# More slack for seven kinds of step in a list-scheduled graph network kernel

## The chip, the cores and the metric

The kernel runs on one core of a Trainium2 chip. The time is the device time of one execution in microseconds, as the median of several runs. Five engines take part, each with its own in-order queue of instructions: TensorE (PE in the profile, its weight loads PEld), VectorE (DVE), ScalarE (ACT), GpSimd (POOL) and SyncE (SP, which here only issues DMAs).

## The reference

There are 16 batches of 1024 nodes with 64 channels and one 1024 x 1024 adjacency matrix each. Four layers follow each other, each of the form `x = layernorm(x + layer(x))`:

```python
x = _layernorm(x + _L0_gnn_ref(x, adj, nodemask, ...))   # quantiles over the neighbours, then an MLP
x = _layernorm(x + _L1_gnn_ref(x, adj, weight, bias))    # adj @ (x @ weight) + bias
x = _layernorm(x + _L2_gnn_ref(x, adj, W1, W2, GCN_W))   # (softmax(x W (x W)^T) + adj) @ x, gelu
x = _layernorm(x + _L3_gnn_ref(x, adj, nodemask, ...))   # quantiles again
```

The quantile layers are the costly ones. For each node with more than 10 neighbours the edges whose rank is one certain multiple are removed, from both sides. What is left gives a list of neighbours for each node. For each node and channel the values of the neighbours are sorted, and the quantiles 0.25, 0.5 and 0.75, each interpolated between two ranks, are added with weights 0.25, 0.5 and 0.25.

## The kernel before

The kernel sorts, for each batch, the nodes by degree. The nodes of highest degree (the first 128, the hubs) have long lists; the other 896 have at most 22 neighbours, by 128-node tiles with capacities 22, 16, 13, 11, 10, 9 and 8 (`TILE_CAPS`).

Seven streams of work, written as Python generators, are merged into one program by `give_out` (line 211). A stream yields one instruction at a time, a `Step`. Each step has an engine, a cost from a table of estimates (`Queue.times`, line 183), and the names of the tiles it reads and writes. At every turn `give_out` looks at the next step of each stream, works out when its inputs are ready and when its engine is free by these estimates, and gives out the one that would start first. `.after(slack)` adds to the ready time for this choice alone: the step counts as ready that many nanoseconds later, so other streams' steps on the same engine go ahead of it if they have some, and the estimated start that is booked does not hold the slack. The order in which steps are given out is the order of each engine's queue; the semaphores between engines follow from it. As all instructions are emitted from the helper at line 180, nearly every line of the profile reads L180, and groups are told apart by tile names.

The streams:

- `graph_stream` (1657): for each batch `graph` (964). `neighbours` (994) loads the matrix by tiles, turns it, counts degrees into `pm` and computes `mi` (half the degree) from it. Then a loop over 8 tiles follows: `counted(t)` gives the running count of neighbours by matmuls into `pq`, ScalarE takes `v` = |pq + mid|, VectorE tests it into `gone`, and further matmuls subtract and transpose `gone`. `both_ways` and `order` make the symmetric graph and the order by degree. `lists` (1102) makes the neighbour lists: 32 tests `hot` for the hubs, whose result is `k.hidx`; for each of the 7 tiles of short lists, matmuls into `pk`, from which VectorE takes the 8 greatest keys at a time (`top`, `rest`) into `k.idx`. The graphs of batches run up to `KEPT` = 5 ahead.
- `fetch_stream` (1287), all of GpSimd: per layer 60 gathers of hub rows (`hrows`, 30 pairs, in 8 buffers), 89 gathers of short-list rows (`rows0`, `rows1`, `rows2`, one buffer each), and 9 scatters of the layer's sums (`sums`), those of one layer in the midst of the next layer's gathers.
- `turn_stream` (1323): transposes each pair of hub rows on TensorE into a bank `turned`, four pairs to a bank, and ScalarE copies the bank to `cols`. At the end of a layer it transposes `tot`, the hubs' result, to `hagg`.
- `sort_stream` (1377), VectorE: sorting networks of `min` and `max` over `cols` (the hubs; weighted sums of them give `tot`), then over `rows0` to `rows2`.
- `pick_stream` (1391): ScalarE scales the sorted rows by the quantile weights, TensorE adds them up in `picked`, and ScalarE copies to `agg`.
- `weight_stream` (1355): loads of the hubs' weights, `hw`.
- `middle_stream` (1639): what follows the quantiles. `last_step` (1519) loads `sums` as `ag`, adds x, transposes by halves (`ot`), runs the two MLP matmuls (`ht`, then into `py`), and makes `z`, the mask and the norm from `py` on VectorE. For the first quantile layer the two middle layers follow (`spread_layer`, `attention_layer`), whose result x3 goes to the table that the second quantile layer gathers from. `layernorm` (942) has one step on ScalarE, the square root `ln_r`, whose result VectorE inverts into `ln_q`.

The 32 quantile layers (two for each batch) are run through in one sequence, the second layer of a batch `LAG` = 2 batches after its first.

Of the kernel before, what the change touches and what calls it, by code (L numbers as in the profile page):

```python
# [16 lines left out]
ALU = mybir.AluOpType  # L17
# [766 lines left out]
def listed_path(ctx: ExitStack, tc: tile.TileContext, x, adj, nodemask,  # L784
# [3 lines left out]
    B, N, C = x.shape  # L788
    H = l0_w1.shape[1]
    P = 128  # L790
    NT = N // P
# [3 lines left out]
    V, A, T, G = nc.vector, nc.scalar, nc.tensor, nc.gpsimd  # L795
# [10 lines left out]
    ident = const.tile([P, P], F32, name="ident")  # L806
# [129 lines left out]
    V, A, T, G, D = (Queue(c, e) for c, e in zip("VATGD", (nc.vector, nc.scalar, nc.tensor, nc.gpsimd, nc.sync)))  # L936
# [5 lines left out]
    def layernorm(z, sq, y):  # L942
        s = small["t"].tile([P, NT], F32, name="ln_s")
        yield V.tensor_reduce(s, z, AX.X, ALU.add)
        mean = small["t"].tile([P, NT], F32, name="ln_mean")
        yield V.tensor_scalar(mean, s, 1.0 / C, None, ALU.mult)
        yield V.tensor_tensor(z, z, mean.unsqueeze(2).to_broadcast([P, NT, C]), ALU.subtract)
        yield V.tensor_mul(sq, z, z)
        v = small["t"].tile([P, NT], F32, name="ln_v")
        yield V.tensor_reduce(v, sq, AX.X, ALU.add)  # L950
        yield V.tensor_scalar(v, v, 1.0 / C, EPS, ALU.mult, ALU.add)
        r = small["t"].tile([P, NT], F32, name="ln_r")
        yield A.activation(r, v, AF.Sqrt)

        q = small["t"].tile([P, NT], F32, name="ln_q")
        yield V.reciprocal(q, r)
        yield V.tensor_mul(q, q, v)
        yield V.tensor_add(q, q, r)
        yield V.tensor_scalar(q, q, 0.5, None, ALU.mult)
        yield V.reciprocal(q, q)  # L960
        yield V.tensor_mul(y, z, q.unsqueeze(2).to_broadcast([P, NT, C]))
        return y
# [31 lines left out]
    def neighbours(np, psn, b, k, near, nbt):  # L994
        k.adjt = dram.tile([NH, NT, P, HALF], F32, name="adjt", bufs=3)
        for t in range(NT):
            mine = slice(t * P, (t + 1) * P)
            a = np.tile([P, N], F32, name="a", bufs=3)
            yield D.dma_start(a, adj[b, mine, :])
            nb = np.tile([P, N], F16, name="nb", tag="h", bufs=3)  # L1000
            yield V.tensor_scalar(nb, a, 0.0, None, ALU.is_gt)
            yield V.tensor_mul(nb[:, mine], nb[:, mine], noteye)
            pa = two(psn, [P, NT, P])
            for j in range(NT):
                yield T.transpose(pa[:, j, :], a[:, j * P:(j + 1) * P], ident)
            at = np.tile([P, NT, P], F32, name="at", bufs=2)
            yield A.copy(at, pa)
            h, c0 = t // (HALF // P), t % (HALF // P) * P
            yield A.dma_start(k.adjt[h, :, :, c0:c0 + P].rearrange("j p n -> p j n"), at)
            pb = psn.tile([P, NT, P], F16, name="one")  # L1010
            for j in range(NT):
                yield T.transpose(pb[:, j, :], nb[:, j * P:(j + 1) * P], ident16)
            yield A.copy(nbt[:, :, mine], pb)
        pm = psn.tile([P, NT], F32, name="one")
        for t in range(NT):
            for j in range(NT):
                yield T.matmul(pm[:, t:t + 1], nbt[:, j, t * P:(t + 1) * P], ones16[:, 0:1],
                         start=(j == 0), stop=(j == NT - 1))


        mi = small["g"].tile([P, NT], I32, name="mi")
        yield V.tensor_scalar(mi, pm, 1.0, None, ALU.add)
        do = small["g"].tile([P, NT], F32, name="do")
        yield V.scalar_tensor_tensor(do, pm, 10.0, k.mask, ALU.is_gt, ALU.mult)
        yield V.tensor_scalar(mi, mi, 1, None, ALU.logical_shift_right)
        mid = small["g"].tile([P, NT], F32, name="mid")
        yield V.tensor_scalar(mid, mi, -1.5, -1024.0, ALU.mult, ALU.add)
        off = small["g"].tile([P, NT], F32, name="off")
        yield V.tensor_scalar(off, mi, 0.5, 1.0, ALU.mult, ALU.add)
        yield V.tensor_mul(off, off, do)  # L1030
        yield V.tensor_scalar(off, off, -1.0, None, ALU.add)
        def counted(t):
            pq = two(psn, [P, NH, HALF])
            for h in range(NH):
                last = (h + 1) * (HALF // P) - 1
                for j in range(last + 1):
                    c0 = max(j * P, h * HALF)
                    yield T.matmul(pq[:, h, c0 - h * HALF:], nbt[:, j, t * P:(t + 1) * P],
                                   run[:, c0 - j * P:(h + 1) * HALF - j * P], start=(j == 0), stop=(j == last))
            return pq  # L1040

        pq = yield from counted(0)
        for t in range(NT):
            mine = slice(t * P, (t + 1) * P)
            v = np.tile([P, N], F16, name="v", tag="h", bufs=3)
            yield A.activation(v, pq.rearrange("p h n -> p (h n)"), AF.Abs, bias=mid[:, t:t + 1])
            gone = np.tile([P, N], F16, name="gone", tag="h", bufs=3)
            yield V.tensor_scalar(gone, v, off[:, t:t + 1], None, ALU.is_equal)
            if t + 1 < NT:
                pq = yield from counted(t + 1)  # L1050

            for h in range(NH):
                pn = psn.tile([P, HALF], F32, name="one")
                yield T.matmul(pn, neg16, gone[:, h * HALF:(h + 1) * HALF], start=True, stop=False)
                for j in range(HALF // P):
                    yield T.matmul(pn[:, j * P:(j + 1) * P], nbt[:, h * (HALF // P) + j, mine], ident16,
                                   start=False, stop=(j == HALF // P - 1))
                yield A.copy(near[:, t, h * HALF:(h + 1) * HALF], pn)
            pg = psn.tile([P, NT, P], F16, name="pg", tag="one")
            for j in range(NT):  # L1060
                yield T.transpose(pg[:, j, :], gone[:, j * P:(j + 1) * P], ident16)
            yield A.copy(nbt[:, :, mine], pg)
# [39 lines left out]
    def lists(lp, psl, b, near, perm, deg, k):  # L1102
# [35 lines left out]
        pi = psl.tile([CH, 2, 2 * HC], F32, name="pi", tag="one")  # L1138
# [9 lines left out]
        pi = psl.tile([P, 2, NG], F32, name="pi2", tag="one")  # L1148
        for q in range(GC):
            yield T.matmul(pi, quarter[:, q], named.rearrange("s h (g q) -> s q h g", q=GC)[:, q],  # L1150
                           start=(q == 0), stop=(q == GC - 1))
        yield V.tensor_copy(k.hidx, pi)
        events.add(("hidx", b))


        for g in range(1, NT):
            pk = psl.tile([P, NH, HALF], F32, name="two")
            for h in range(NH):
                cols = slice(h * HALF, (h + 1) * HALF)
                yield T.matmul(pk[:, h], ones16[0:1, :], key_row[:, cols], start=True, stop=False)  # L1160
                for t in range(NT):
                    yield T.matmul(pk[:, h], perm[:, t, g * P:(g + 1) * P], near[:, t, cols],
                             start=False, stop=(t == NT - 1))
            cap = TILE_CAPS[g - 1]
            top = lp.tile([P, MOST + 2], F32, name="top", bufs=2)
            keys = pk.rearrange("p h n -> p (h n)")
            for r in range((cap + 7) // 8):
                yield V.max(out=top[:, 8 * r:8 * r + 8], in_=keys)
                if 8 * r + 8 < cap:
                    rest = lp.tile([P, N], F32, name="rest", bufs=2)  # L1170
                    yield V.match_replace(out=rest, in_to_replace=top[:, 8 * r:8 * r + 8], in_values=keys,
                                    imm_value=-4096.0)
                    keys = rest
            yield V.tensor_scalar(k.idx[:, g - 1, :cap], top[:, :cap], 0.0, None, ALU.max)
# [148 lines left out]
    def turn_stream():  # L1323
        for n, (l, b) in enumerate(layers):
            k = batches[b]
            yield Wait("hidx", b)
            k.cols = [None, None]
            for g in range(0, NG, 4):
                pt = psh.tile([P, 4 * P], F32, name="turned")
                for i in range(g, min(g + 4, NG)):  # L1330
                    yield Wait("h", n, i)
                    e = min(P, (2 * HC - i * GC) * CH)
                    yield T.transpose(pt[:, (i - g) * P:(i - g) * P + e], k.hrows[i][:e].rearrange("p h c -> p (h c)"),
                                      ident[:e, :e]).after(3000)
                events.add(("turned", n, g // 4))
                first, end = g * GC, min((g + 4) * GC, 2 * HC)
                for i in range(2):
# [181 lines left out]
    def last_step(n, l, b, k):  # L1519
# [21 lines left out]
                c0 = t % (HALF // P) * P  # L1541
                yield T.matmul(py[:, t, :], ht[:, c0:c0 + P], w2, start=True, stop=True)
        z = features("z")
        yield V.tensor_tensor(z, py, b2.unsqueeze(1).to_broadcast([P, NT, C]), ALU.add)
        yield V.tensor_mul(z, z, k.mask.unsqueeze(2).to_broadcast([P, NT, C]))
        yield V.tensor_add(z, z, xn)
        return (yield from layernorm(z, ag, features("y")))
# [166 lines left out]
```

## Time and profile before

| | us |
|---|---|
| median of 3 runs | 8266.02 |
| lowest and highest | 8259.21 and 8276.33 |
| the profiled execution | 8298.99 |
| its span, first to last instruction | 8297.2 |

| engine | busy, us | share of the span |
|---|---|---|
| TensorE | 5196.2 | 63% |
| VectorE | 7057.9 | 85% |
| ScalarE | 2329.8 | 28% |
| GpSimd | 5693.1 | 69% |

The mean granted clock of TensorE was 0.738 of full speed. A layer takes 232 to 262 us after the first two, told by the first gather of each layer's hub rows; layers with graph work beside them alternate between about 236 and 260 us, and those after the last graph (from 7000 us on) take 226 to 247 us.

A line of groups gives: engine, operation, out<-in by tile names, shapes and count; then busy time in us and the mean of one in ns; then the engine's idle time ahead of these instructions in us and what ended most of it. A line of waits gives: who waited, for whom, how long in total, how many times, and the longest. A line of the timeline gives start, length, engine, instruction, and in brackets the idle time ahead of it and its releaser.

### The profile page before, as it was taken

The numbers are of one execution on the slowest core, as the hardware profiler recorded it, in microseconds if no ns is written. First come the engines' busy times: TensorE is split into PE (matmuls) and PEld (weight loads), VectorE is DVE, ScalarE is ACT, GpSimd is POOL, SyncE is SP. The second block draws the span as 40 slices with busy tenths as digits, with TensorE's granted clock in tenths as the row PEclk, the third lists the DMA queues.
The fourth block names the chain that finished last, engine by engine and source line by source line (L and its number), as shares of the span: only waits on it lengthen the run. The fifth ranks groups of instructions, "written<-read, shape, count | busy, mean of one in ns | idle before, by whom it ended". The sixth has DMA issues, their size and how long they took to land. (4 is left out here: it accounts for less than half of the span.)

```text
span 8297.2 us, 81388 instructions
## 1 busy us (share of the span) xinstructions
PE 5196.2 (63%) x24851; PEld 2751.4 (33%) x24851; DVE 7057.9 (85%) x14774; ACT 2329.8 (28%) x5554; POOL 5693.1 (69%) x5087
## 2 busy tenths in 40 slices
PE   6568777758475675856658575665856668272541
PEld 4244333333332333433233333323333233131221
DVE  2779798789898898988889898898988889979795
ACT  3324334142322324132242313324232232121121
POOL 0734677667776776767767676777767777777774
PEclk8778887878686776877778686777867678565565
DMA  1331423232323222232322324222332222232221
GB/s 48 72 72 50 99 44 97 46 77 65 73 50 89 52 55 69 62 81 52 63 63 66 73 50 94 52 51 69 72 71 52 65 61 65 33 68 33 58 42 22
DMA packets 762008, 513.78 MB, mean 62 GB/s; under 512 B 459098, under 2 KB 600538, under 8 KB 761306
## 3 DMA queue, kind: packets, MB, share of 16 engines
q1 hardware_dynamic: 457434, 261.99, 13.0%
q0 software_dynamic: 161792, 163.90, 11.6%
q10 hardware_dynamic: 142336, 82.59, 3.4%
q8 instruction: 201, 3.29, 0.2%
q14 instruction: 245, 2.01, 0.1%
HBM read 408.73 MB, written 103.55 MB: 62 GB/s over the span
## 5 line engine op out<-in xcount | busy, mean ns | idle before, releaser
L180 POOL DMA_INDIRECT rows<-table,idx x2848 | 3264.6, 1146 | 867.9 <-issue 841.1
L180 POOL DMA_INDIRECT hrows<-table,hidx x1920 | 2096.4, 1092 | 928.8 <-issue 443.1
L180 DVE TENSOR_TENSOR spare<-cols 128x528 f32<-128x528 f32 (+11 forms) x1632 | 1057.1, 674 | 71.4 <-ACT cols L180 47.7
L180 DVE TENSOR_TENSOR cols<-spare 128x528 f32<-128x528 f32 (+11 forms) x1664 | 1074.8, 680 | 15.8
L180 PE MATMUL picked<-rows,ident 128*128 128x64 f32 (+2 forms) x2496 | 646.1, 366 | 347.6 <-ACT rows L180 346.6
L180 PE MATMUL turned<-ident,hrows 128*128 128x128 f32 x960 | 343.1, 379 | 673.6 <-DMA hrows<-table,hidx 636.3
L180 POOL DMA_INDIRECT sums<-agg,node x224 | 260.2, 1162 | 665.2 <-DMA sums<-agg,node 195.3
L180 ACT ACTIVATE rows<-rows,wt 128x64 f32<-128x64 f32 x2272 | 612.5, 340 | 191.2 <-DVE rows L180 188.5
L180 PEld LDWEIGHTS picked<-rows,ident 128*128 128x128 f32 x2496 | 479.7, 244 | 543.1 <-ACT rows L180 446.3
L180 PE MATMUL pi<-hot,numbers 128*32 128x236 f16 x4096 | 549.4, 284 | 76.0 <-DVE hot L180 74.4
L180 DVE TENSOR_TENSOR spare<-rows 128x64 f32<-128x64 f32 (+8 forms) x1056 | 539.0, 541 | 58.1 <-DMA sums<-hagg,hnode 21.7
L180 PE MATMUL two<-near,perm 128*128 128x512 f16 x1792 | 544.6, 459 | 0.0
L180 PEld LDWEIGHTS <-numbers 128*32 128x32 f16 x4096 | 397.0, 103 | 331.8 <-issue 275.7
L180 ACT COPY cols<-turned 128x512 f32<-128x512 f32 (+3 forms) x288 | 148.5, 528 | 1253.8 <-PE turned L180 1252.9
L180 PE MATMUL two<-run,nbt 128*128 128x512 f16 (+3 forms) x1536 | 408.9, 438 | 142.4 <-ACT v L180 142.4
L180 PEld LDWEIGHTS turned<-ident,hrows 128*128 128x128 f32 x960 | 163.4, 175 | 926.5 <-issue 591.9
L180 PEld LDWEIGHTS <-nbt 128*128 128x128 f16 x3584 | 303.6, 113 | 491.4 <-issue 416.9
L180 DVE TENSOR_TENSOR rows<-spare 128x512 f32<-128x512 f32 (+9 forms) x896 | 462.5, 538 | 0.8
L180 PE MATMUL turned<-ident,tot 128*64 128x128 f32 x32 | 11.7, 365 | 609.4 <-DVE tot L180 609.4
L180 DVE TENSOR_TENSOR spare<-cols,spare 128x472 f32<-128x472 f32 (+2 forms) x704 | 379.2, 539 | 15.6
L180 PE MATMUL one<-xt,wt 64*128 64x512 f32 x512 | 369.8, 851 | 22.0 <-DVE top L180 22.0
L180 DVE TENSOR_TENSOR rows<-rows,spare 128x64 f32<-128x64 f32 (+4 forms) x1120 | 363.2, 329 | 17.6
(232 smaller groups left out, 10079.9 us busy)
## 6 DMA issues: line engine op xcount, KB each, us to landing
at<-adjt SPq DMA_DIRECT2D x512, 256.0 KB
a<-in_adj_dram SPq DMA_DIRECT2D x128, 512.0 KB
adjt<-at ACTq DMA_DIRECT2D x128, 512.0 KB
rows<-table,idx POOLq DMA_INDIRECT x2848
hrows<-table,hidx POOLq DMA_INDIRECT x1920
hw<-hwt SPq DMA_DIRECT2D x64, 472.0 KB
hwt<-ho ACTq DMA_DIRECT2D x64, 236.0 KB
ag<-sums SPq DMA_DIRECT2D x32, 256.0 KB
```

The source lines that it names most:

```text
L180: return Step(lambda: f(*args, **kw), self.engine, cost, late, reads, writes, "dma" in name)
```

## The change

The change adds a slack to six kinds of VectorE steps, and doubles the slack that the hub transpositions already had on TensorE. Nothing else differs.

```diff
@@ layernorm
-        yield V.reciprocal(q, r)
+        yield V.reciprocal(q, r).after(1000)
@@ neighbours
-        yield V.tensor_scalar(mi, pm, 1.0, None, ALU.add)
+        yield V.tensor_scalar(mi, pm, 1.0, None, ALU.add).after(3000)
...
-            yield V.tensor_scalar(gone, v, off[:, t:t + 1], None, ALU.is_equal)
+            yield V.tensor_scalar(gone, v, off[:, t:t + 1], None, ALU.is_equal).after(2000)
@@ lists
-        yield V.tensor_copy(k.hidx, pi)
+        yield V.tensor_copy(k.hidx, pi).after(3000)
...
-                yield V.max(out=top[:, 8 * r:8 * r + 8], in_=keys)
+                yield V.max(out=top[:, 8 * r:8 * r + 8], in_=keys).after(0 if r else 1500)
@@ turn_stream
                     yield T.transpose(pt[:, (i - g) * P:(i - g) * P + e], k.hrows[i][:e].rearrange("p h c -> p (h c)"),
-                                      ident[:e, :e]).after(3000)
+                                      ident[:e, :e]).after(6000)
@@ last_step
-        yield V.tensor_tensor(z, py, b2.unsqueeze(1).to_broadcast([P, NT, C]), ALU.add)
+        yield V.tensor_tensor(z, py, b2.unsqueeze(1).to_broadcast([P, NT, C]), ALU.add).after(6000)
```

## The prediction

> **What bounds the kernel now.** I read the busy shares first, then the idle time of VectorE by group, then the waits of VectorE and GpSimd in the even middle of the run (1000 to 6750 us, which is 1380 of the 1920 hub gathers, so 23 of 32 layers, 250 us each), and last one wait in the timeline.
>
> ```profile
> PE 5196.2 (63%) x24851; PEld 2751.4 (33%) x24851; DVE 7057.9 (85%) x14774; ACT 2329.8 (28%) x5554; POOL 5693.1 (69%) x5087
> ...
> L180 POOL DMA_INDIRECT rows<-table,idx x2848 | 3264.6, 1146 | 867.9 <-issue 841.1
> L180 POOL DMA_INDIRECT hrows<-table,hidx x1920 | 2096.4, 1092 | 928.8 <-issue 443.1
> ```
>
> VectorE leads, but GpSimd is as full as it: beside 5693 us busy it has 841 + 443 us of "issue", about 0.3 us ahead of each gather, in which it waits for nothing. Together 84%.
>
> ```profile
> L180 DVE TENSOR_SCALAR gone<-v,off 128x1024 f16<-128x1024 f16 x128 | 65.1, 509 | 251.1 <-ACT v L180 251.1
> L180 DVE TENSOR_TENSOR z<-one,b 128x512 f32<-128x512 f32 x32 | 22.1, 689 | 222.0 <-PE one L180 222.0
> L180 DVE MAX8 top<-two 128x8 f32<-128x1024 f32 x112 | 137.6, 1228 | 151.7 <-PE two L180 151.6
> L180 DVE CAST hidx<-pi 128x60 uint32<-128x60 f32 x16 | 3.5, 219 | 53.2 <-PE pi L180 53.2
> L180 DVE TENSOR_SCALAR mi<-one 128x8 int32<-128x8 f32 x16 | 2.6, 162 | 26.9 <-PE one L180 26.9
> L180 DVE RECIPROCAL ln_q<-ln_r 128x8 f32<-128x8 f32 x64 | 12.4, 193 | 15.3 <-ACT ln_r L180 15.3
> ```
>
> VectorE's idle time is 8297 − 7058 = 1239 us; 720 us of it stand ahead of these six groups, and they are the six VectorE steps that the change defers. For rows that GpSimd has to fetch VectorE waits next to nothing, so sorting work is nearly always there to fill a gap.
>
> ```profile
> POOL sums L180 <- DMA sums<-agg,node: 135.9, 74, 3.2
> POOL hrows L180 <- PE turned L180: 124.8, 63, 23.7
> POOL sums L180 <- ACT agg L180: 90.1, 16, 12.6
> POOL sums L180 <- DMA sums<-hagg,hnode: 70.1, 23, 5.4
> POOL hrows L180 <- DMA hrows<-table,hidx: 57.6, 189, 0.3
> POOL sums L180 <- ACT rows L180: 48.4, 27, 9.2
> ```
>
> These are GpSimd's waits from 1000 to 6750 us. The scatters wait for each other (136 + 70) and keep doing so. What a faster VectorE can give back: 209 us for late sorts and picks (90 + 48, and in the rest of that view 29 + 15 + 13 + 8 + 4 + 1 on VectorE's rows, cols, spare, z, top and hd) and 139 us for hub buffers not yet turned (125 + 14). So GpSimd cannot get under 5750 − 348 = 5402 us there, 235 us a layer.
>
> ```profile
> 4104.30 0.45 PE L180 MATMUL turned<-ident,hrows 128*128 128x128 f32 x1 [2.73 <-DMA hrows<-table,hidx]
> 4107.32 0.44 PE L180 MATMUL turned<-ident,hrows 128*128 128x128 f32 x1 [2.58 <-DMA hrows<-table,hidx]
> 4110.32 0.45 PE L180 MATMUL turned<-ident,hrows 128*128 128x128 f32 x1 [2.56 <-DMA hrows<-table,hidx]
> 4113.55 0.47 PE L180 MATMUL turned<-ident,hrows 128*128 128x128 f32 x1 [2.78 <-DMA hrows<-table,hidx]
> ...
> 4127.04 0.69 DVE L180 TENSOR_TENSOR z<-one,b 128x512 f32<-128x512 f32 x1 [14.13 <-PE one L180]
> ```
>
> Here is the worst wait: the last step's matmuls stand on TensorE behind hub transpositions that wait, one by one, for gathers 2.5 to 3 us apart; 14 us later z can start, and VectorE stood still for it. Twelve of the 32 z waits are of 14 to 18 us, 179 us together.
>
> **The change, part by part.** No instruction is added or removed; instructions of each kind are as many in both built programs, table loads of ScalarE (50) too. GpSimd's stream is a single one and keeps its order. What moves is the order on VectorE, TensorE, ScalarE and SyncE. For the VectorE steps I counted, in both built orders, the VectorE work that stands between the producer and the step, with durations from the trace's groups (a 128x512 f32 operation 0.68 us, and so on), and took from each traced wait the added cover, never more than the wait.
>
> Graph test (gone): cover 1.3 us before, 2.8 after; a traced wait is 251/128 = 2.0 us. Instance by instance 127 us go. The eight tests of the first graph wait 8 us each with nothing else to run and keep it.
>
> z: cover 0.9 before, 6.2 after. That alone takes 94 us (222 to 128; the last z, 13 us, has no cover). But the transpositions' larger slack acts on the same wait: between the add of ag and z stand 18 hub transpositions in every other layer before, 7 after. In the stretch above, five of them cost 13.4 us between ot (done at 4102.3) and the next matmul (4115.7); after, one stands there. I take 195 us: all but the last z and some 14 us. Bounds 94 and 209.
>
> First maximum (top): cover 0.3 to 1.4; 27 us, of 152, since the slack only helps where hub or sorting work is ready and the first graph (about 30 us) has none. As TensorE will stand less behind waiting transpositions I take 45; bounds 27 and 120.
>
> hidx 29 us (cover 0.5 to 2.8), mi 18 (0.4 to 3.0), ln_q 11 (0.5 to 1.5).
>
> Hub transpositions: TensorE waits 636 us for their gathers. The order has 5 gathers (median) between a row pair's second gather and its transposition before, 7 after: 2 x (1.09 + 0.3) = 2.8 us more. At a mean wait of 636/351 = 1.8 us most of these waits go. TensorE is at 63%, so this is worth nothing by itself beyond z and top. Its price: 8 row-pair buffers are 16 gathers, the transposition has 7 instead of 9 gathers' time (9.7 for 12.5 us) before the refill is held up.
>
> Late next: hidx is 400 us or more ahead of its first gather from the sixth batch on (at 4406 us for a layer whose gathers begin at 4821); in batches 1 and 2 only 27 us, where the order leaves VectorE's work ahead of it unchanged or 8 us less. The x3 that follows z is some 470 us ahead of its layer, in the last one 32 us: there the tail can gain no more than that. SyncE's loads move too; VectorE waits for them 45 us (nb) and 19 us (ag), nearly all before 100 us and at the end: 0 ± 20. ScalarE is busy for 28%; its copies to cols, which wait 1253 us for TensorE, come later with the transpositions and so hold up the row scalings behind them less: again 0, and up to 20 us either way.
>
> Sum on VectorE: 127 + 195 + 45 + 29 + 18 + 11 = 425 us, bounds 306 and 514.
>
> Of this the span gets what GpSimd can follow. In the middle 366 of VectorE's 557 us of waits go, two thirds. Late sorts also move up: the last operation of a network stands 7 to 18 us of VectorE work earlier in most layers, because graph work is put behind it. So I let 80% of the 209 us go, 167; of the 139 us for hub buffers 40%, since VectorE's tot comes sooner but the transpositions themselves later: 55. That is 222 us, 240 us a layer. From 6750 us on GpSimd has 45 us of such waits: 20. From 0 to 1000 us, where the graph sets the pace, 35 of VectorE's 56 us after the first graph. Sum 277.
>
> The profiled execution took 8299.0 us (span 8297.2), 33 us over the median of the runs, 8266.0. 8299 − 277 = 8022, or 3.3% less; on the median 7990.
>
> One more price: gathers take 940 ns at best and 1146 in the mean. If that difference comes from a busy VectorE, 425 us less idle time touch 425/1.45 = 293 gathers with 0.2 us, 60 us on GpSimd; if not, 0. I take 0 and keep 60 for the range. The Trainium skill (SBUF — State Buffer, "Who interferes with whom") speaks against the change here: a VectorE operation in a two-port mode locks GpSimd out while it makes descriptors. By the same section tensor_tensor, which is what fills the gaps, has no such mode, so its price would be 0; by the row above it would be up to 60 us, 8050 for 7990.
>
> **The rivals.** *GpSimd follows wholly:* all 348 us of the middle go, 60 elsewhere: 408, 7860. For it: 94% of GpSimd's middle is already work. Against: two engines bound through eight buffers and one set of rows each never both run without waits.
>
> *GpSimd binds at once:* VectorE's waits go, but hub buffers come free later and only the 209 us shrink, by half: 105 and 25 elsewhere, 130: 8136. For it: TensorE waits 344 us in the middle for tot, 15 times and 23 us each, over the 9.7 us that the buffers bear.
>
> *Slower:* TensorE's long graph strings push each deferred group of four transpositions past the buffers' 9.7 us, and GpSimd stops for 2.8 us more each time. There are 32 x 15 = 480 groups; it decides from 277/2.8 = 99 of them. At one in four, 120 x 2.8 = 336: 59 us slower, 8325. Against: GpSimd now meets "PE turned" 99 times with 177 us, and that wait is TensorE's for tot, which comes earlier.
>
> *Nothing is ready when steps are deferred,* so the order stays: 8266. The built order speaks against it, except for the first graph.
>
> **How the numbers follow.** Forecast 7990 (7900 to 8080): 0.52. GpSimd follows wholly: 0.14. It binds at once: 0.20. No change, 0.2% or 17 us either way, which is about what this kernel's measurement can tell: 0.03. Slower: 0.11. Faster is 0.86. The range 7850 to 8200 leaves out the far part of the first rival, the weak end of the second, and the slower case.
>
> **What would show it.** Right: idle ahead of gone near 125 us, z under 40, top near 100; TensorE's wait for hub gathers well below 636; layers of 240 us in the middle; GpSimd's waits on ACT agg and rows down to a fifth. Wrong: "hrows <- PE turned" above 177 us by hundreds (the slower case), or VectorE's idle time moved to waits for rows or cols (GpSimd binds).

## The result: 0.5% slower

| | before | after |
|---|---|---|
| median, us (7 runs each) | 8266.99 | 8318.82 |
| lowest and highest | 8258.16 and 8280.46 | 8294.75 and 8327.80 |
| the profiled execution, and its span | 8298.99, 8297.2 | 8327.80, 8326.0 |

The ratio is 1.005, with a 95% interval of 1.0037 to 1.0062. The forecast was 7990 us. The traced execution of before was 32 us above its median and that of after 9 us above, so the traces differ by 29 us where the medians differ by 52: what follows by layers is known to some 20 us.

The page of after, engines and two groups (columns as before):

```profile
PE 5267.4 (63%) x24851; PEld 2776.8 (33%) x24851; DVE 7057.6 (85%) x14774; ACT 2319.1 (28%) x5554; POOL 5694.7 (68%) x5087
...
L180 POOL DMA_INDIRECT hrows<-table,hidx x1920 | 2053.9, 1070 | 1079.6 <-issue 458.3
...
L180 PE MATMUL turned<-ident,hrows 128*128 128x128 f32 x960 | 356.1, 392 | 773.7 <-DMA hrows<-table,hidx 697.9
```

The last group in before:

```profile
L180 PE MATMUL turned<-ident,hrows 128*128 128x128 f32 x960 | 343.1, 379 | 673.6 <-DMA hrows<-table,hidx 636.3
```

The work of VectorE and GpSimd is the same to 2 us. What grew is waiting: GpSimd's idle time ahead of hub gathers from 929 to 1080 us, and TensorE's wait for those gathers from 636 to 698, which had been expected to shrink. TensorE's own work also grew, by 71 us, at a mean granted clock of 0.733 in the trace of after for 0.738 in that of before. Whether that adds to the time no run separates; e10 below, at 0.736 and with 47 us more of that work than before, was faster than before.

VectorE's groups in after:

```profile
L180 DVE MAX8 top<-two 128x8 f32<-128x1024 f32 x112 | 137.6, 1228 | 181.0 <-PE two L180 181.0
L180 DVE TENSOR_SCALAR gone<-v,off 128x1024 f16<-128x1024 f16 x128 | 63.8, 499 | 118.8 <-ACT v L180 118.5
L180 DVE TENSOR_TENSOR slot<-two,minus 128x128 f16<-128x128 f32 (+6 forms) x128 | 41.2, 398 | 75.4 <-PE two L180 75.4
L180 DVE TENSOR_TENSOR z<-one,b 128x512 f32<-128x512 f32 x32 | 22.0, 689 | 156.2 <-PE one L180 156.2
L180 DVE COPY mask<-one 128x8 f32<-128x8 f32 x16 | 2.6, 163 | 57.4 <-PE one L180 57.4
L180 DVE RECIPROCAL ln_q<-ln_r 128x8 f32<-128x8 f32 x64 | 12.6, 196 | 38.3 <-ACT ln_r L180 38.2
L180 DVE TENSOR_SCALAR mi<-one 128x8 int32<-128x8 f32 x16 | 2.5, 159 | 9.0 <-PE one L180 9.0
L180 DVE CAST hidx<-pi 128x60 uint32<-128x60 f32 x16 | 3.4, 214 | 8.8 <-PE pi L180 8.8
```

Two of them, slot (a step of the lists) and mask, in before:

```profile
L180 DVE TENSOR_TENSOR slot<-two,minus 128x128 f16<-128x128 f32 (+6 forms) x128 | 41.1, 398 | 16.0 <-PE two L180 16.0
L180 DVE COPY mask<-one 128x8 f32<-128x8 f32 x16 | 2.6, 162 | 8.6 <-PE one L180 8.5
```

The test gone lost 132 us of wait, z only 66, and top gained 29. With hidx (53.2 to 8.8), mi (26.9 to 9.0) and ln_q (15.3 to 38.3) the six groups stand at 512 us after 720. But slot went from 16.0 to 75.4, mask from 8.6 to 57.4, and others followed: VectorE's idle time in all is 8326 - 7058 = 1268 us, 29 more than before. The waits have moved.

GpSimd's waits in after, from 1000 to 6750 us (who, for whom, us in total, times, longest):

```profile
POOL hrows L180 <- PE turned L180: 225.0, 69, 44.8
POOL sums L180 <- DMA sums<-agg,node: 95.9, 59, 3.8
POOL sums L180 <- DMA sums<-hagg,hnode: 39.4, 23, 3.6
...
POOL sums L180 <- ACT rows L180: 31.5, 18, 6.4
```

Picks do come sooner: ACT rows fell from 48 to 31 us, and ACT agg, 90 us before, is no longer in this view. But the scatters' waits put down to VectorE's spare and nb rose, from 13 to 38 and from none to 30, so that of the 209 us for late sorts and picks 151 are left. The scatters' waits for each other fell, from 206 to 135. And the wait for hub buffers rose by 100 us, from 125 to 225; with the stop of layer 17, which before is put down to "PE one" (13.0) and after to "issue" (25.8), by 112. Over the whole run "hrows <- PE turned" went from 177 to 315.

By the first gather of each layer's hub rows, the span falls into three parts:

| span, us | to layer 7 | layers 7 to 27 | from layer 28 | all |
|---|---|---|---|---|
| before | 2090 | 5200 | 1008 | 8297 |
| after | 2134 | 5181 | 1011 | 8326 |

The first seven layers lose 44 us; the twenty-one layers behind them gain 19, not clear of the 20 above, where some 200 were expected. Of the first seven, layer 1 went from 343 to 372 us and layer 5 from 284 to 299 (the range of 232 to 262 given ahead for before leaves out layers 2, 5 and 25, of 218, 284 and 264).

**Where GpSimd stops.** In the middle, every other layer (7, 9, 11 and so on to 25) took 256 to 264 us before, those between them 232 to 237, about the 235 that the prediction worked out for GpSimd alone. The long layers begin with a stop. Here is that of layer 15, whose first gather starts at 4068 us before and at 4105 after; the timeline of before, then that of after (start, length, engine, instruction, idle time ahead and its releaser):

```profile
4090.16 1.08 POOL L180 DMA_INDIRECT hrows<-table,hidx  x1 [0.31 <-issue]
...
4097.45 0.42 PE L180 MATMUL turned<-ident,tot 128*64 128x128 f32 x1 [37.73 <-DVE tot L180]
...
4098.97 1.45 POOL L180 DMA_INDIRECT hrows<-table,hidx  x1 [7.73 <-PE turned L180]
```

```profile
4126.73 0.95 POOL L180 DMA_INDIRECT hrows<-table,hidx  x1 [0.30 <-issue]
...
4139.25 1.23 DVE L180 TENSOR_REDUCE tot<-cols 128x20 f32<-128x640 f32 x1
...
4140.54 0.42 PE L180 MATMUL turned<-ident,tot 128*64 128x128 f32 x1 [26.12 <-DVE tot L180]
4141.31 1.12 PE L180 MATMUL turned<-ident,hrows 128*128 128x128 f32 x4 [0.35 <-ACT hagg L180]
4142.06 0.94 POOL L180 DMA_INDIRECT hrows<-table,hidx  x1 [14.38 <-PE turned L180]
```

The one stream of hub transpositions puts layer 15's behind the transposition of layer 14's tot. Until tot is sorted none of them runs, the eight buffers are full after 22 us of gathers, and GpSimd stands. Tot was turned 29 us after layer 15's first gather before, 35 after: the stop is 14.4 us for 7.7. In the layers of that kind tot is turned 29 to 35 us after the first gather before and 35 to 46 after; in the others it is turned up to 9 us after it before, and no more than 1 us after it with the change. VectorE's order has changed with it: of its work outside the sorting networks the traces have 90 and 33 us in alternate intervals between two tots before, 101 and 23 after. That this makes tot late is argued, not shown (see e1).

### The profile page after: what moved, and what is told of

Its sections match the earlier page's. It is cut to its first block, busy times and chain, and to the rows that moved or that the text cites. A ratio compares the mean times of both kernels' runs of the same rounds, so it can differ in the third digit from the quotient of the medians.

```text
span 8326.0 us, 81277 instructions
## 1 busy us (share of the span) xinstructions
PE 5267.4 (63%) x24851; PEld 2776.8 (33%) x24851; DVE 7057.6 (85%) x14774; ACT 2319.1 (28%) x5554; POOL 5694.7 (68%) x5087
## 5 line engine op out<-in xcount | busy, mean ns | idle before, releaser
L180 POOL DMA_INDIRECT rows<-table,idx x2848 | 3310.9, 1163 | 867.9 <-issue 838.4
L180 POOL DMA_INDIRECT hrows<-table,hidx x1920 | 2053.9, 1070 | 1079.6 <-issue 458.3
L180 DVE TENSOR_TENSOR spare<-spare 128x64 f32<-128x64 f32 (+7 forms) x512 | 363.6, 710 | 13.9
L180 DVE TENSOR_SCALAR hot<-slot 128x1888 f16<-128x1888 f16 x512 | 339.3, 663 | 38.7 <-PE pi L180 38.4
```

The costliest lines, as they stand in the source:

```text
L180: return Step(lambda: f(*args, **kw), self.engine, cost, late, reads, writes, "dma" in name)
```

## The experiments

Each ratio is to the kernel before on the same chip, with its 95% interval; e1 to e4, e5 to e8 and e9 to e12 shared a chip each, with before at 8269, 8285 and 8290 us.

**Which part, with 8 buffers: e1 and e2.** e1 is after with the hub transpositions' slack put back, e2 before with that slack alone.

```diff
-                                      ident[:e, :e]).after(6000)
+                                      ident[:e, :e]).after(3000)
```

> All six VectorE slacks, hub transpositions back at their old slack. Theory T (late tot): the VectorE slacks push graph work in front of tot in every other layer, GpSimd's 8 row-pair buffers run full and it stops; the built order has the same 13 us shift of work between layers as the changed kernel, so the time stays at 8300 to 8330 us and the hub buffers' wait (hrows <- PE turned) near 300. Rival B (buffers held longer): the deferred transpositions are the loss; without them the wait goes back to some 180 us and the time falls to 8130 to 8220. Rival C (TensorE is the pace, filled waits only move on): 8260 to 8320, with waits of VectorE as long as before.

> Only the hub transpositions' slack is doubled. Theory T: tot moves by 2 us of work only, so 8255 to 8290. Rival B: all the price and none of the gain, 8350 to 8400, with the wait for hub buffers over 300 us. Rival C: within 0.2% of 8267.

e1: 8276.33 us, 1.0002 (0.9989 to 1.0015). e2: 8272.04, 1.0007 (0.9996 to 1.0019). Neither part alone moves the time, and only both together lose. "hrows <- PE turned" was 185.6 us in e1 and 199.3 in e2, against 315.0 with both. In layers 7 to 27 they gain 56 and 60 us by their traces, of which 21 and 42 us may be only that the trace of before is a long one; e1 gives 38 back and e2 13 before layer 7. So the slower transpositions are not by themselves the cause, nor are the six VectorE slacks. For theory T e1 is a miss: its traced work between tots alternates as in after (101 and 23 us), yet tot is turned only 26 to 33 us after the first gather in layers 7, 9 and up to 27, and their stops are 93 us, for 204 in after and 108 before. So the shift alone doesn't make tot late: in e1 GpSimd comes to those layers later instead, as the layers between take 244 us for 236 in after. Rival C fits e1 and e2.

**Do the buffers hold the gain? e3 and e4.** Sixteen buffers in place of eight, without the change and with it.

```diff
-HROWS = 8
+HROWS = 16
```

> The kernel before, with 16 row-pair buffers in place of 8, so that GpSimd can run 44 us ahead of the first transposition and not 22. Theory T: tot is turned 30 to 35 us after the layer's first gather in every other layer, so the stops of 8 to 24 us in layers 5 to 27, 132 us in all, go: 8130 to 8190. Rival B: the same or less, 8130 to 8230. Rival C: 8250 to 8280, as what GpSimd does not lose there it loses in its scatters.

> The changed kernel with 16 buffers. Theory T: its stops of 14 to 45 us, 249 us in layers 5 to 27, go almost all (tot comes 35 to 46 us after the first gather), and VectorE's filled waits count at last: 8070 to 8150, under the kernel before with 16 buffers. Rival B: about the same as the kernel before with 16 buffers. Rival C: 50 us above it.

e3: 8166.99, 0.9875 (0.9855 to 0.9896). e4: 8118.9, 0.9817 (0.9799 to 0.9835). Both as theory T expected, and rival C is out: more depth alone is worth 1.2%, and with it the change is worth 0.6% more instead of costing 0.5%. Layers 7 to 27 take 5088 us in e3 and 5004 in e4: the change's gain there is 84 us, though the trace of e4 is 23 us above its median, against 19 with eight buffers. The group of z in e3, then in e4:

```profile
L180 DVE TENSOR_TENSOR z<-one,b 128x512 f32<-128x512 f32 x32 | 22.1, 690 | 133.6 <-PE one L180 133.6
```

```profile
L180 DVE TENSOR_TENSOR z<-one,b 128x512 f32<-128x512 f32 x32 | 22.0, 686 | 32.2 <-PE one L180 32.2
```

The z that was forecast under 40 us is there once GpSimd no longer stops and the slacks are given. With eight buffers the gathers start again late, and the matmuls of the last step stand behind transpositions that wait for them one by one, as in the stretch that the prediction showed: in the 25 us ahead of that z TensorE waits 10 to 13 us for hub gathers in after, 0 to 2.5 in e4 (layers 7, 9 and up to 27).

**Which slack pays with 16 buffers, and where: e5 to e8.** e5 is e4, with the graph slacks (mi, gone, hidx, top) for the fifth graph and later alone; e6 has only the graph slacks, e7 only those of z, ln_q and the hub transpositions. e8 is e5 with eight buffers.

```diff
-            yield V.tensor_scalar(gone, v, off[:, t:t + 1], None, ALU.is_equal).after(2000)
+            yield V.tensor_scalar(gone, v, off[:, t:t + 1], None, ALU.is_equal).after(2000 if b > 3 else 0)
```

> The changed kernel with 16 buffers, and the four graph slacks (mi, gone, hidx, top) given from the fifth batch on only. Theory E (the early graphs are the pace, nothing is there to run in their stead, so deferring them only delays the lists and tot): layers 1, 4 and 5, which took 373, 260 and 284 us with the slacks and 340, 250 and 266 without, go back, and the time is 8050 to 8085. Rival (those layers lose by z and the hub slack): 8105 to 8130, no change from 8119.

> Only the four graph slacks, with 16 buffers. Theory E with the steady gain by z: layers 1 and 5 are as slow as with all slacks, z keeps its 134 us of waits, and the time is at or above that of the kernel before with 16 buffers, 8150 to 8190. Rival (the gain of the 16-buffer pair comes from the graph tests, 118 us less idle): 8110 to 8140.

> Only the slacks of z, ln_q and the hub transpositions, with 16 buffers. Theory E: the early layers keep their 340 and 266 us, z's wait falls from 134 to some 30 us, 8080 to 8130. Rival (gain by the graph tests): 8150 to 8175.

> The changed kernel, 8 buffers, with the graph slacks from the fifth batch on only. Theory E: layer 1 falls from 372 to some 343 us and layer 5 from 299 to some 284, and the time is 8260 to 8290; the steady layers keep their stops for hub buffers, so it is not faster than before. Rival (the whole loss lies in the steady layers): 8305 to 8330.

e5: 8150.73, 0.9835 (0.9822 to 0.9848), a miss: the early layers still took 2109 us, so the slacks of the first four graphs are not all of that loss. e6: 8200.91, 0.9901 (0.9882 to 0.992). e7: 8148.21, 0.9828 (0.9809 to 0.9846). e8: 8308.9, 1.0027 (1.0018 to 1.0037). e7 and e8 missed too, 18 and 19 us above theory E's ranges; layer 1 took 360 and 358 us for some 340 expected. e8's time is that of its rival, the whole loss in the steady layers, against which e10 speaks. The graph slacks cut gone's wait to 105 us in e6 and gain nothing over e3 (0.9875); those of z, ln_q and the hub transpositions leave gone at 256 in e7 and gain. A large wait removed is not a large gain.

**All slack late: e9 and e10.** As e5 and e8, with the slacks of z, ln_q and the hub transpositions left out of the first seven layers too, and the graph slacks from the sixth graph on.

```diff
-                                      ident[:e, :e]).after(6000)
+                                      ident[:e, :e]).after(6000 if n > 6 else 3000)
...
-        yield V.tensor_tensor(z, py, b2.unsqueeze(1).to_broadcast([P, NT, C]), ALU.add).after(6000)
+        yield V.tensor_tensor(z, py, b2.unsqueeze(1).to_broadcast([P, NT, C]), ALU.add).after(6000 if n > 6 else 0)
```

> The changed kernel with 16 buffers and every one of the seven slacks given only after the first seven layers (graphs from the sixth batch on). Theory F (any of the slacks costs the first layers 45 to 60 us, whichever it is, as in the two halves run alone, and the later layers gain 84 us by all of them): the first layers to layer 6 take 2065 us as without slacks, not 2110 to 2124, and the time is 8070 to 8100. Rival (the first layers' difference is not due to the slacks, or the later gain depends on it): 8115 to 8150.

> The same with 8 buffers. Theory F: first layers as before, 2089 us instead of 2135, later layers 5165 to 5185 us against 5198 before, so 8235 to 8270, at best a little under the kernel before. Rival: 8290 to 8330.

e9, with 16 buffers: 8102.67, 0.9774 (0.9761 to 0.9787), the fastest of the runs on these three chips and better than both kernels, though 3 us above its range on a chip where before took 21 us more than on that of e1 to e4. e10, with eight: 8264.64, 0.9965 (0.9953 to 0.9977). This settles the sign. e10 is the change without its early slacks; it takes 2078 us to layer 7 where after takes 2134, both take 5181 from there to layer 27, and the spans differ by 55 us, as do those 56. e8, with the early slacks of z, ln_q, the transpositions and the fifth graph, takes 2110: by these single traces some 32 us are theirs and 24 those of the first four graphs. In e10 the stops in layers 7, 9 and up to 27 are 205 us, as in after; in e9 they are under 2.

Where the early loss lies can be read in the traces. In layer 1 GpSimd waits for that layer's own picks (ACT rows and agg) 124 to 132 us in the five runs that have the slacks of the first four graphs (after, e1, e4, e6, e12), and 100 to 114 in the nine that have not (before, e2, e3, e5, e7 to e11). Layer 5's stop for hub buffers is 44 and 45 us with these slacks and 15 to 24 without (eight buffers), or 25 to 48 and 0 to 4 (sixteen). The stops in layers 0 to 4, with eight buffers, are 72 to 82 us where the transpositions have their slack early (after, e2, e8) and 30 to 42 where not (before, e1, e10, e11). Layer 5's stop isn't tot's doing in after: tot is turned 6 us after the first gather there, and the transpositions stand behind matmuls for the lists of a graph:

```profile
1596.53 0.30 PE L180 MATMUL turned<-ident,tot 128*64 128x128 f32 x1 [0.77 <-DVE tot L180]
...
1653.08 1.90 PE L180 MATMUL two<-near,perm 128*128 128x512 f16 x8
1654.82 0.60 PE L180 MATMUL turned<-ident,hrows 128*128 128x128 f32 x4
1655.36 0.94 POOL L180 DMA_INDIRECT hrows<-table,hidx  x1 [44.79 <-PE turned L180]
```

**Is it tot, or the depth? e11 and e12.** e11 is before with tot's transposition in a stream of its own and in a bank of the middle stream, so that it no longer holds the next layer's. e12 is e4 without the hub transpositions' slack.

```diff
+    def tot_stream():
+        for n, (l, b) in enumerate(layers):
+            k = batches[b]
             yield Wait("hubdone", n)
-            pt = psh.tile([64, P], F32, name="turned")
+            pt = one([64, P])
             yield T.transpose(pt, k.tot, ident)
```

> The kernel before, 8 buffers, with the transposition of tot taken out of the stream of hub transpositions into one of its own (into a bank of the middle stream), so that those of the next layer need not stand behind it on TensorE. Theory T (late tot at the head of TensorE's queue is what holds the hub buffers): the stops of 8 to 24 us go as they did with 16 buffers, hub buffers' wait under 60 us, 8150 to 8200. Rival (too few buffers whatever stands ahead): the wait stays at 180 us, 8255 to 8280.

> The six VectorE slacks without the hub transpositions' one, with 16 buffers. If the transpositions' slack is what shortens z's wait beyond its cover, z waits 80 to 130 us and not 32, and the time lies between the 16-buffer kernels before and after, 8130 to 8160. If z's own slack does it, z is near 32 us and the time within 0.2% of 8119.

e11: 8225.38, 0.992 (0.9906 to 0.9933), between the two theories. Its waits, of TensorE, then of GpSimd:

```profile
PE turned L180 <- DMA hrows<-table,hidx: 875.5, 347, 20.5
```

```profile
POOL sums L180 <- ACT rows L180: 271.6, 39, 48.5
...
POOL hrows L180 <- PE turned L180: 78.0, 72, 23.9
```

The wait "hrows <- PE turned" fell from 177 to 78 us. The stops in layers 7, 9 and up to 27, 108 us before, are gone, which shows that these came from tot's place in that stream and its bank (the run moves both at once); what is left lies in the first six layers, 24 us of it in layer 5. So tot's place in the order is worth about two thirds of what 16 buffers bring (0.8 of 1.25%). The rest goes to other waits: the transpositions now go ahead and wait for gathers (636 to 876 us), and picks come later (186 to 272). e12: 8216.38, 0.9906 (0.9893 to 0.992), worse than expected and than e3 (on another chip): z stands at 165.6 us. With 16 buffers the six VectorE slacks gain nothing unless the hub transpositions have theirs, which is what shortens z's wait (32.2 us in e4).

**Two points once more: e13 to e18.** e13 and e14 hold the graph slacks, or those of z, ln_q and the transpositions, in the early layers alone. e15 puts tot's transposition at the head of the picks, and e16 does so with the slacks of e10.

```diff
@@ e13
+            yield V.tensor_scalar(gone, v, off[:, t:t + 1], None, ALU.is_equal).after(2000 if b <= 4 else 0)
@@ e14
+                                      ident[:e, :e]).after(3000 if n > 6 else 6000)
@@ e15, e16: in pick_stream, ahead of its loop over TILE_GROUPS
+            yield Wait("hubdone", n)
+            pt = psp.tile([64, P], F32, name="picked")
+            yield T.transpose(pt, k.tot, ident)
```

> Before (8 buffers) with the slacks of mi, gone, hidx and top for the first five graphs alone; everything else as before. What it tells apart: which of the change's parts costs the first layers the 44 to 56 us (layer 7's first gather at 2134 us with the whole change, 2090 before, 2078 with the slacks only late). Theory G, the graph slacks let network and last-step work ahead of a graph that is just in time: layer 7's first gather at 2115 to 2140 us, and the whole 25 to 50 us above before. Rival S, the hub transpositions' and z's slack does it: within 12 us of before.

> Before with the slacks of z, ln_q and the hub transpositions in the first seven layers alone; the graph steps and everything later as before. Theory G: within 12 us of before, layer 7's first gather at 2080 to 2100 us. Rival S: 25 to 50 us above before, layer 7's first gather at 2115 to 2140. If the two parts share the loss, 10 to 30 us in each run.

> Before (8 buffers), with tot's transposition taken out of the stream of hub transpositions and put at the head of the stream of picks, into a bank of its own, so that the next layer's hub transpositions no longer stand behind tot. Theory T, tot's place in TensorE's order is what stops the gathers: GpSimd's waits 'hrows <- PE turned' fall from 177 us to under 60, and 8150 to 8205 us on a chip with before at 8270 to 8290 (ratio 0.985 to 0.991). Rival, depth of buffers counts for itself: the waits fall but the time stays above 0.994.

> The change with its slacks in the later layers alone (8 buffers, ratio 0.9965) and tot's transposition at the head of the picks. Theory T, the change's later gain is lost because it puts work ahead of tot, behind which the hub transpositions stand: with tot out of their way the slacks gain 50 to 90 us over the run before this one (as they do with 16 buffers: 0.9875 to 0.9774), ratio 0.975 to 0.982. Rival, the deferred transpositions themselves hold up the 8 buffers: under 30 us below the run before this one, ratio above 0.984.

> The kernel of e15 once more, because on the chip of e13 to e16 the kernel before took 9685 us instead of 8270 to 8290 and TensorE stood 646 to 1056 us in 'issue', against 3 us in the trace of before, so that those ratios cannot be set beside the others. Theory T: 'hrows <- PE turned' under 60 us and a ratio of 0.985 to 0.991. Rival, depth of buffers counts for itself: a ratio above 0.994.

> The kernel of e16 once more, for the same reason. Theory T: 50 to 90 us under the run before this one, ratio 0.975 to 0.982. Rival, the deferred transpositions themselves hold up the 8 buffers: under 30 us below it, ratio above 0.984.

These six ran on two other chips, where the kernel before itself took 9685 us (e13 to e16) and 9987 us (e17, e18). TensorE's waits in e13:

```profile
PE one L180 <- issue: 487.9, 261, 44.9
```

There TensorE stands without waiting for anything that the profile shows, 1056 us in all in e13, against 3 us in the trace of before, which is from another chip. The ratios were 1.0355 (1.0279 to 1.0431) for e13, 1.0174 (1.0097 to 1.0252) for e14, 0.9742 (0.9679 to 0.9805) for e15, 0.954 (0.9463 to 0.9617) for e16, 0.9751 (0.9685 to 0.9817) for e17 and 0.9663 (0.9607 to 0.9719) for e18. The directions agree with the earlier runs: both early parts lose, tot out of the way gains, and the late slacks gain on top of it, in the second pair with intervals that overlap. But the sizes are another chip's: hub-buffer waits were 516 us in e15 and 651 in e17, not under 60, so theory T's mark was not met. The second pair differs by 0.9% where the first differs by 2.1%. Whether tot alone, or the transpositions themselves, hold the later gain at eight buffers stays open for a chip like the first three.

## Why the prediction was wrong

**The terms on VectorE** were sized from each traced wait alone. gone (127; 132) and mi (18; 18) came about as said, and hidx (29; 44) by more. z (195; 66) failed, since its larger half, 101 us beyond the cover of 94, counted on hub transpositions that would no longer wait for gathers; those gathers started later, TensorE's wait for them rose, and not even the 94 came. top (45; 29 lost) and ln_q (11; 23 lost) went the other way. And the sum left out that other steps would come to wait for the same engines, slot and mask above all: 208 us went from the six groups and 237 came up elsewhere.

**The step that failed first** is the hub buffers: "that wait is TensorE's for tot, which comes earlier". It came later, in just the layers in which GpSimd stops. I had counted the work ahead of the last operation of a network layer by layer and taken 7 to 18 us less as a common gain; it holds for every second layer, those in which GpSimd is the pace and gains nothing. In the others more of VectorE's other work stands ahead of tot, which e1 shows to be not enough by itself. So the wait went 100 us up in the middle where 55 down were booked. Nor was all of that wait TensorE's for tot: of the 177 us before, 24 were layer 5's stop behind a graph's matmuls. The picks' 167 us were partly right: ACT agg and rows, 138 us, fell to 31, but all waits for sorts and picks only from 209 to 151.

**The step that gave the sign** is the term of 35 us gained from 0 to 1000 us and "late next": hidx was seen just 27 us ahead in batches 1 and 2, with the work ahead of it "unchanged or 8 us less", and costed at nothing. The slacks in the first seven layers cost 56 us instead, as e10 shows. It was not hidx: GpSimd waits for it once in either trace, ahead of the very first gather. What came late with the early graph slacks were the picks of layer 1, for which GpSimd waits before layer 2's gathers (104 us, then 128), and layer 5's transpositions (a stop of 24 us, then 45); with the early transposition slack those of layers 0 to 4 (stops of 33 us, then 72). Which one of the graph slacks does it stays open.

**The conversion** of VectorE's sum into span by shares (80% and 40%) had no row behind it. In the layers where GpSimd sets the pace VectorE's waits rose, from 12 to 18 us a layer to 18 to 28. In the eleven others (7, 9, up to 27) they fell by 103 us, from 347 to 244. That is the saving that could have paid, but in the same layers the stops for hub buffers grew by 96 us, from 108 to 204, and these layers became only 24 us shorter.

**The slower rival** had the right mark ("above 177": 315) and nearly the right time (8325; 8319), but another place: not each group of four deferred transpositions, 480 times 2.8 us, but one stop in every second layer behind tot. That its time came so near is luck: e2 shows that the deferred transpositions alone leave the time as it was. The weight on it, 0.11, was too small: the evidence, 23 us waits for tot against a margin of 9.7, stood in the prediction, under "GpSimd binds at once".

**The 60 us for gathers** beside a fuller VectorE stay unsettled. (The shortest gather in the trace of before takes 905 ns, not 940.) The Trainium skill (SBUF — State Buffer, "Who interferes with whom") gives tensor_tensor no two-port mode, but also has it contend with GpSimd's reads when both its inputs are in SBUF, which the prediction left out in putting the price at 0. After has no fuller VectorE to test it. e3, with VectorE idle for 135 us less than before, has both kinds of gathers together at 5361 us as before, which agrees; e9, with 196 less, has 5412. But e7, with 149 less, has 5333, and e12, with 58 less, 5444, so the gathers' time doesn't follow VectorE's idle time in these runs.

What stays open: why e1 and e2 each gain in layers 7 to 27 (56 and 60 us by the traces, 35 and 18 if the long trace of before is allowed for) and both together nothing clear of that. Tot's lateness in the stopping layers is the one thing seen to differ. e11 shows that tot's place makes the stops in before; that it alone takes the change's later gain is not shown, as the runs that should have isolated it ran on the two other chips.

## What to carry to other kernels

Before a wait is priced, find which engine sets the pace in each stage and each kind of layer: idle time ahead of a step pays nothing where another engine is the pace, and a slack that pays in the steady layers can cost in the first ones. In a list-scheduled kernel a slack moves other work as well; look at what that work is put in front of, above all a step behind which an in-order queue holds the refill of buffers. Here the deeper buffers came first (1.2%), then slack in the later layers alone (e9: 2.3% in all).

## What the runs showed of the hardware

Chips differ for this kernel. Three gave 8269, 8285 and 8290 us for the kernel before, and two gave 9685 and 9987 us. On these two no trace of before was taken; in those of e13 to e18 TensorE stands in "issue" for 646 to 1074 us (e16 and e17) against 3 us in the trace of before, at a granted clock of 0.70 to 0.71 against 0.74. GpSimd's gathers there took no longer (rows 1104 ns in e13 for 1146 in before, in the mean), so its waits, not its work, grew. What holds TensorE's instructions there isn't known.
